# Two groups at a time in the attention layers of a graph network, and gated weights set up behind them

## The chip, the cores and the metric

The kernel runs on one core of one Trainium2 chip. The metric is the device time of one execution in microseconds (us), the median of three runs. A core has five engines with a queue of instructions each: TensorE (PE in the profile; PEld are its weight loads), VectorE (DVE), ScalarE (ACT), GpSimd (POOL) and SyncE (SP), which here starts the transfers.[...] TensorE writes into PSUM, which has eight banks of 128 x 512 floats; the other data stand in SBUF.

## The reference, cut to what matters

128 graphs of 128 nodes, 256 features per node. Three attention layers, then one gated layer of three steps, all with a residual:

```python
# three times, with layer's own W and a (the third also multiplies h' by nodemask)
h  = maximum(layernorm(x), 0)
Wh = einsum('bnf,fo->bno', h, W)
e  = (Wh @ a1)[:, :, None] + (Wh @ a2)[:, None, :]
e  = where(e > 0, e, 0.2 * e)
att = softmax(where(adj > 0, e, -9e15), axis=-1)
x  = x + elu(einsum('bij,bjo->bio', att, Wh))

# gated layer
h = maximum(layernorm(x), 0)
for i in range(3):
    m    = einsum('bnd,de->bne', h, weight[i])
    aggr = einsum('bst,bsd->btd', adj != 0, m)
    r = sigmoid(aggr @ w_ih_r.T + b + h @ w_hh_r.T + b)   # z in the same way
    n = tanh(aggr @ w_ih_n.T + b + r * (h @ w_hh_n.T + b))
    h = (1 - z) * n + z * h
x = x + h
```

All is float32.

## The kernel before

Four graphs make a group (G = 4, T = 512 columns); there are 32 groups. `gat(g)` is the attention part of a group, `gru(g)` its gated part. Both are generators, and the driver decides in which order the source emits their pieces. A framework builds the dependencies, and its scheduler orders the instructions on each engine; that order is fixed when the program is compiled, and each engine follows it. Pools give each tile a fixed number of buffers; a new tile waits until the last reader of the one that had its buffer is done.

```python
grp = ctx.enter_context(tc.tile_pool(name="grp", bufs=2))
gw = ctx.enter_context(tc.tile_pool(name="gw", bufs=2))
BANKS = {"gat": 3, "gru": 4, "tr": 1}          # the eight PSUM banks

loaded = {0: load(0)}                          # x and adj of group 0
# ... W of the three layers, with two more columns W @ a1 and W @ a2 (VectorE) ...
# ... nodemask, transposed (nmp) ...

def transposed(src, dst, nm_):                 # weights: load, transpose, copy
    t = su.tile([P, rows, D], FT, tag="wld", name=f"{nm_}_ld")
    nc.sync.dma_start(t, src.rearrange("(r p) d -> p r d", p=P))
    # ... nc.tensor.transpose into bank("gat"), nc.vector.tensor_copy out of it ...
transposed(w_hh, whh, "whh")
transposed(w_ih, wih, "wih")
for i in range(STEPS):
    transposed(gweight[i], gt, f"gt{i}")
    # wc[i] = gweight[i] @ w_ih.T: 8 matmuls of 384 columns (wcp), 4 copies by VectorE
# ... biases ...
```

One attention layer. The names are those of the profile:

```python
def attention(g, l, xt, cap):
    nm, rs = stats(xt, name)                   # VectorE statistics; rs: power on GpSimd
    for b in range(G):
        nc.scalar.activation(xn[:, b, :], xt[:, b, :], AF.Relu, bias=nm[:, b : b + 1])
    hT = turned(xn, gw, "hT", name)            # hTp: 8 transposes; k=0 copied by ScalarE, k=1 by VectorE
    yield
    for c in range(G):                         # whp: 2 matmuls of 258 columns each
        nc.tensor.matmul(ps[:, :E], hT[:, k, c * P : (c + 1) * P], W[l][:, k, :], ...)
        nc.scalar.activation(wh[:, c, :], ps[:, :E], AF.Copy, scale=rs[:, c : c + 1])
    yield
    # e: 4 transposes; em: 4 + 1 operations and nmx on VectorE; pe: 4 exponentials on
    # ScalarE; ri and pe * ri on VectorE
    xm = gw.tile([P, G, D], FT, tag="xm", name=f"xm_{name}")
    nc.gpsimd.tensor_scalar(xm, xt, 1.0, -1.0, op0=OP.mult, op1=OP.add)
    yield
    # atp: 4 transposes of pe, at: copied by VectorE
    xo = grp.tile([P, G, D], FT, tag=f"x{l + 1}", name=f"xo_{name}", bufs=3 if l == 2 else 2)
    for j in range(G // 2):                    # hp: 2 matmuls of 256 columns each
        nc.tensor.matmul(hp[:, b * D : (b + 1) * D], at[...], wh[:, c, :D], ...)
        nc.scalar.activation(t, hp, AF.Exp)
        nc.vector.scalar_tensor_tensor(u, hp, 0.0, xm[...], op0=OP.max, op1=OP.add)
        nc.vector.scalar_tensor_tensor(xo[...], t, 1.0, u, op0=OP.min, op1=OP.add)
    yield xo
```

After three layers `gat` makes the gated layer's first input (statistics, `hn`, eight transposes hTp). A gated step, for each half c of the features:

```python
if c == 0: evac(0)                             # hnp: 4 transposes of h in the bank "tr", hn: copied by ScalarE
for k in range(KD):
    mm(nn, cn, whh, h, k, ...); mm(pr, cr, whh, h, k, ...); mm(pz, cz, whh, h, k, ...)
    if c == 0:
        aggregate(k)                           # agp: 4 matmuls in the bank "tr", ag: copied by VectorE
        if k == 0: evac(1)
# wn; then r <- ag, n; ni <- ag, n, tanh; z <- ag; d, d, h: two matmuls of 512 columns
# for each gate, activations on ScalarE, five operations of 128x512 on VectorE
```

The driver:

```python
AHEAD = 2
for g in range(min(AHEAD, NG)):
    run(gat(g))
for g in range(NG):
    run(gru(g))
    if g + AHEAD < NG:
        run(gat(g + AHEAD))
```

In the profile a float32 matmul shows as two instructions (48 agp instructions in a group are 24 matmuls), a transpose as one.

Of the kernel before, what the change touches and what calls it, by code (L numbers as in the profile page):

```python
# [8 lines left out]
FT = mybir.dt.float32  # L9
I32 = mybir.dt.int32  # L10
AF = mybir.ActivationFunctionType
OP = mybir.AluOpType
AX = mybir.AxisListType

P = 128
# [6 lines left out]
def kernel(  # L22
# [24 lines left out]
    nc = tc.nc  # L47
    B, N, D = x.shape
    KD = D // P
    G = 4  # L50
# [16 lines left out]
    def load(g):  # L67
        xt = grp.tile([P, G, D], FT, tag="x0", name=f"x_{g}")
        nc.sync.dma_start(xt, x[g * G : (g + 1) * G].rearrange("b n d -> n b d"))
        at = grp.tile([P, G, N], I32, tag="adj", name=f"adj_{g}")  # L70
        nc.sync.dma_start(at, adj[g * G : (g + 1) * G].rearrange("b i j -> i b j"))
        return xt, at

    loaded = {0: load(0)}


    ident = const.tile([P, P], FT, name="ident")
# [25 lines left out]
    nc.tensor.transpose(nmp[:, :B], nm, ident[:B, :B])  # L103
    nmT = const.tile([P, B], FT, name="nmT")
    nc.vector.tensor_copy(nmT, nmp[:, :B])


    def transposed(src, dst, nm_):
        rows = src.shape[0] // P
        t = su.tile([P, rows, D], FT, tag="wld", name=f"{nm_}_ld")  # L110
        nc.sync.dma_start(t, src.rearrange("(r p) d -> p r d", p=P))
        for k in range(KD):
            for r0 in range(0, rows, 4):
                n = min(4, rows - r0)
                ps = bank("gat", f"{nm_}_{k}_{r0}")
                for r in range(n):
                    nc.tensor.transpose(
                        ps[:, r * P : (r + 1) * P], t[:, r0 + r, k * P : (k + 1) * P], ident
                    )
                nc.vector.tensor_copy(dst[:, k, r0 * P : (r0 + n) * P], ps[:, : n * P])  # L120

    O3 = w_ih.shape[0]
    NCH = O3 // P
    whh = const.tile([P, KD, O3], FT, name="whh")
    transposed(w_hh, whh, "whh")

    nc.vector.tensor_scalar_mul(whh[:, :, 2 * D :], whh[:, :, 2 * D :], 0.5)
    wih = su.tile([P, KD, O3], FT, tag="wih", name="wih", bufs=1)
    transposed(w_ih, wih, "wih")

    wc = []
    for i in range(STEPS):
        gt = su.tile([P, KD, D], FT, tag="gt", name=f"gt_{i}")
        transposed(gweight[i], gt, f"gt{i}")
        wci = const.tile([P, KD, O3], FT, name=f"wc_{i}")
        for m in range(KD):
            for o0 in range(0, O3, 384):
                ps = bank("gat", f"wcp_{i}_{m}_{o0}")
                for k in range(KD):
                    nc.tensor.matmul(  # L140
                        ps[:, :384], gt[:, k, m * P : (m + 1) * P], wih[:, k, o0 : o0 + 384],
                        start=(k == 0), stop=(k == KD - 1),
                    )
                nc.vector.tensor_copy(wci[:, m, o0 : o0 + 384], ps[:, :384])
        wc.append(wci)


    bi = const.tile([P, NCH], FT, name="bi")
    bh = const.tile([P, NCH], FT, name="bh")
    with nc.allow_non_contiguous_dma(reason="768 biases, once"):  # L150
        nc.sync.dma_start(bi, b_ih.rearrange("(c p) -> p c", p=P))
        nc.sync.dma_start(bh, b_hh.rearrange("(c p) -> p c", p=P))
    brz = const.tile([P, NCH], FT, name="brz")
    nc.vector.tensor_add(brz, bi, bh)
    nc.vector.tensor_scalar_mul(brz, brz, 0.5)
    nc.vector.tensor_scalar_mul(bh, bh, 0.5)

    setup.close()
    rw = ctx.enter_context(tc.tile_pool(name="rw", bufs=2))


    def stats(xt, name):
# [29 lines left out]
    def attention(g, l, xt, cap):  # L192

        name = f"{g}_{l}"
        nm, rs = stats(xt, name)

        xn = gw.tile([P, G, D], FT, tag="xn", name=f"xn_{name}")
        for b in range(G):
            nc.scalar.activation(xn[:, b, :], xt[:, b, :], AF.Relu, bias=nm[:, b : b + 1])
        hT = turned(xn, gw, "hT", name)  # L200
        yield

        wh = gw.tile([P, G, E], FT, tag="wh", name=f"wh_{name}")
        for c in range(G):
            ps = bank("gat", f"whp_{name}_{c}")
            for k in range(KD):
                nc.tensor.matmul(  # L207
                    ps[:, :E], hT[:, k, c * P : (c + 1) * P], W[l][:, k, :],
                    start=(k == 0), stop=(k == KD - 1),
                )  # L210
            nc.scalar.activation(wh[:, c, :], ps[:, :E], AF.Copy, scale=rs[:, c : c + 1])  # L211
        yield

        e2 = bank("gat", f"e2_{name}")
        for c in range(G):
            nc.tensor.transpose(  # L216
                e2[:, c * P : (c + 1) * P], wh[:, c, D + 1 : D + 2].to_broadcast([P, P]), ident
            )

        em = gw.tile([P, G, N], FT, tag="em", name=f"em_{name}")  # L220
        for c in range(G):
            nc.vector.scalar_tensor_tensor(  # L222
                em[:, c, :], e2[:, c * P : (c + 1) * P], wh[:, c, D : D + 1], cap[:, c, :],
                op0=OP.add, op1=OP.min,
            )
        nc.vector.scalar_tensor_tensor(em, em, ALPHA, em, op0=OP.mult, op1=OP.max)
        nmx = gw.tile([P, G], FT, tag="nmx", name=f"nmx_{name}")
        nc.vector.tensor_reduce(nmx, em, axis=AX.X, op=OP.max, negate=True)
        pe = gw.tile([P, G, N], FT, tag="pe", name=f"pe_{name}")
        sm = gw.tile([P, G], FT, tag="sm", name=f"sm_{name}")  # L230
        for b in range(G):
            nc.scalar.activation(  # L232
                pe[:, b, :], em[:, b, :], AF.Exp, bias=nmx[:, b : b + 1], accum_out=sm[:, b : b + 1]
            )
        ri = gw.tile([P, G], FT, tag="ri", name=f"ri_{name}")
        nc.vector.reciprocal(ri, sm)
        if l == 2:
            nc.vector.tensor_mul(ri, ri, nmT[:, g * G : (g + 1) * G])
        nc.vector.tensor_tensor(
            pe, pe, ri.rearrange("p (g o) -> p g o", o=1).to_broadcast([P, G, N]), op=OP.mult  # L240
        )

        xm = gw.tile([P, G, D], FT, tag="xm", name=f"xm_{name}")
        nc.gpsimd.tensor_scalar(xm, xt, 1.0, -1.0, op0=OP.mult, op1=OP.add)  # L244
        yield
        atp = bank("gat", f"atp_{name}")
        for b in range(G):
            nc.tensor.transpose(atp[:, b * P : (b + 1) * P], pe[:, b, :], ident)  # L248
        at = gw.tile([P, T], FT, tag="at", name=f"at_{name}")
        nc.vector.tensor_copy(at, atp)  # L250
        xo = grp.tile([P, G, D], FT, tag=f"x{l + 1}", name=f"xo_{name}", bufs=3 if l == 2 else 2)
        for j in range(G // 2):
            hp = bank("gat", f"hp_{name}_{j}")
            for b in range(2):
                c = 2 * j + b
                nc.tensor.matmul(  # L256
                    hp[:, b * D : (b + 1) * D], at[:, c * P : (c + 1) * P], wh[:, c, :D],
                    start=True, stop=True,
                )

            t = gw.tile([P, T], FT, tag="t", name=f"t_{name}_{j}")
            nc.scalar.activation(t, hp, AF.Exp)  # L262
            u = gw.tile([P, T], FT, tag="u", name=f"u_{name}_{j}")
            nc.vector.scalar_tensor_tensor(  # L264
                u, hp, 0.0, xm[:, 2 * j : 2 * j + 2, :].rearrange("p b d -> p (b d)"),
                op0=OP.max, op1=OP.add,
            )
            nc.vector.scalar_tensor_tensor(  # L268
                xo[:, 2 * j : 2 * j + 2, :].rearrange("p b d -> p (b d)"), t, 1.0, u,
                op0=OP.min, op1=OP.add,  # L270
            )
        yield xo

    done = {}

    def gat(g):
        xt, adj_t = loaded.pop(g)
        if g + 1 < NG:
            loaded[g + 1] = load(g + 1)
        cap = grp.tile([P, G, N], FT, tag="cap", name=f"cap_{g}")  # L280
        nc.vector.tensor_scalar(cap, adj_t, 0.0, 2.0 * BIG, op0=OP.is_gt, op1=OP.mult)
        nc.vector.tensor_scalar(cap, cap, -BIG, None, op0=OP.add)
        am = grp.tile([P, G, N], FT, tag="am", name=f"am_{g}", bufs=3)
        nc.vector.tensor_scalar(am, adj_t, 0.0, None, op0=OP.not_equal)
        for l in range(3):
            for v in attention(g, l, xt, cap):
                if v is not None:
                    xt = v
                yield
        nm, rs = stats(xt, f"{g}_3")  # L290
        nc.vector.tensor_mul(nm, nm, rs)
        hn = grp.tile([P, G, D], FT, tag="hn0", name=f"hn_{g}_0")
# [103 lines left out]
        nc.sync.dma_start(out[g * G : (g + 1) * G].rearrange("b n d -> n b d"), o)  # L396
        yield

    def run(stream):
        for _ in stream:  # L400
            pass

    AHEAD = 2
    for g in range(min(AHEAD, NG)):
        run(gat(g))
    for g in range(NG):
        run(gru(g))
        if g + AHEAD < NG:  # L410
            run(gat(g + AHEAD))


# [33 lines left out]
```

## Time and profile before

| | |
|---|---|
| time, median of 3 | 3158.22 us (3157.09 to 3161.38) |
| span of the profiled execution | 3155.9 us, 31261 instructions |
| TensorE busy | 3049.1 us (97%) |
| VectorE, ScalarE, GpSimd busy | 57%, 42%, 8% |
| memory traffic | 47.94 MB, mean 15 GB/s |

How to read it: the page gives each engine's busy time, and below it the span in 40 slices of 79 us with a digit each, 9 for 90% or more. PEclk is the clock that TensorE was granted, in tenths of full speed. In the timeline a row is a run of like instructions: start, length, engine, line, operation, tile written <- tiles read, shape, count, and in brackets the idle time of the engine before it with what ended it. An engine's idle time matters where that engine or what waits for it sets the end.

### The profile page before, as it was taken

How to read it: one execution, taken by the hardware profiler on the slowest of the kernel's cores; microseconds unless marked ns; L12 is line 12 of the kernel's file. 1: busy time of each engine (PE TensorE's matmuls, PEld its weight loads, DVE VectorE, ACT ScalarE, POOL GpSimd, SP SyncE). 2: the span in 40 equal slices, each digit the busy share in tenths (PEclk: the TensorE clock that was granted, in tenths of full speed). 3: DMA queues.
4: the chain of work that ended last, by engine and by line, in shares of the span. 5: the costliest groups of instructions: out<-in, count | busy, mean ns of one | idle time of the engine just before them, and what ended most of it. 6: DMA issues, size and time to landing. Idle time of an engine off the chain costs nothing.

```text
span 3155.9 us, 31261 instructions
## 1 busy us (share of the span) xinstructions
PE 3049.1 (97%) x11093; PEld 1730.8 (55%) x11093; DVE 1785.9 (57%) x3960; ACT 1316.4 (42%) x2881; POOL 262.3 (8%) x358
## 2 busy tenths in 40 slices
PE   5799999999999999999999999999999999999999
PEld 3455555555555555555555555555555555555554
DVE  4555565555655555655555655556555555555553
ACT  1344444444444444444444444444444444444442
POOL 0110100010101001100001100101000001010000
PEclk8899999999999999999999999999999999999999
DMA  2000000000000000000000000000000000000000
GB/s 84 11 17 17 11 7 17 17 17 13 15 7 17 17 17 10 14 11 17 17 17 11 7 17 17 17 17 10 7 17 17 17 11 17 7 14 7 7 1 14
DMA packets 56188, 47.94 MB, mean 15 GB/s; under 512 B 3296, under 2 KB 55648, under 8 KB 56032
## 3 DMA queue, kind: packets, MB, share of 16 engines
q1 hardware_dynamic: 56032, 45.95, 4.6%
q8 instruction: 87, 1.43, 0.2%
q14 instruction: 69, 0.57, 0.1%
HBM read 29.17 MB, written 16.78 MB: 15 GB/s over the span
## 4 chain that ended last, share of the span: by engine, by line
PE 79%; DVE 11%; ACT 6%; issue 3%; DMA 1%; POOL 0%; SPq 0%; ACTq 0%; DVEq 0%; POOLq 0%
PE r L321 18%; PE z L321 16%; PE whp L207 10%; PE nn L321 9%; PE ni L321 8%; PE agp L338 4%; PE hTp L183 4%; PE hp L256 4%; DVE st L167 3%; DVE u L264 3%; DVE xo L268 2%; PE hnp L312 2%; PE atp L248 2%; ACT pe L232 2%; PE e L216 1%
## 5 line engine op out<-in xcount | busy, mean ns | idle before, releaser
L321 PE MATMUL r<-ag,wc 128*128 128x512 f32 x768 | 381.3, 597 | 0.0
L321 PE MATMUL ni<-ag,wc 128*128 128x512 f32 x768 | 371.3, 592 | 0.0
L321 PE MATMUL z<-ag,wc 128*128 128x512 f32 x768 | 366.0, 592 | 0.0
L207 PE MATMUL whp<-w,hT 128*128 128x258 f32 x1536 | 361.5, 385 | 0.7 <-ACT hT L187 0.7
L207 PEld LDWEIGHTS whp<-w,hT 128*128 128x128 f32 x1536 | 286.8, 191 | 90.5 <-ACT hT L187 39.1
L222 DVE SCALAR_TENSOR_TENSOR em<-e,wh,cap 128x128 f32<-128x128 f32 x384 | 108.1, 344 | 397.3 <-PE e L216 397.3
L367 ACT ACTIVATE r<-r,brz 128x512 f32<-128x512 f32 x192 | 131.9, 687 | 457.5 <-PE r L321 457.5
L211 ACT ACTIVATE wh<-whp,rs 128x258 f32<-128x258 f32 x384 | 183.0, 477 | 264.9 <-PE whp L207 264.7
L369 DVE SCALAR_TENSOR_TENSOR n<-r,wn 128x512 f32<-128x512 f32 x192 | 130.7, 681 | 263.5 <-ACT r L367 263.5
L362 ACT ACTIVATE wn<-nn,bh 128x512 f32<-128x512 f32 x192 | 131.3, 684 | 326.4 <-PE nn L321 326.4
L321 PE MATMUL nn<-h,whh 128*128 128x512 f32 x512 | 264.8, 599 | 0.0
L321 PE MATMUL z<-h,whh 128*128 128x512 f32 x512 | 263.2, 595 | 0.1
L321 PE MATMUL r<-h,whh 128*128 128x512 f32 x512 | 261.6, 592 | 0.0
L338 PEld LDWEIGHTS agp<-am,hn 128*128 128x128 f32 x1536 | 203.3, 193 | 64.4 <-issue 47.6
L321 PEld LDWEIGHTS z<-ag,wc 128*128 128x128 f32 x768 | 143.5, 190 | 168.0 <-issue 167.9
L374 ACT ACTIVATE n<-n,bi 128x512 f32<-128x512 f32 x192 | 137.8, 718 | 233.6 <-DVE n L373 233.6
L244 POOL TENSOR_SCALAR xm<-xo 128x1024 f32<-128x1024 f32 x64 | 66.9, 1045 | 1965.4 <-DVE xo L268 1965.4
L321 PEld LDWEIGHTS ni<-ag,wc 128*128 128x128 f32 x768 | 140.8, 190 | 153.0 <-issue 153.0
L262 ACT ACTIVATE t<-hp 128x512 f32<-128x512 f32 x192 | 114.6, 597 | 263.4 <-PE hp L256 263.3
L264 DVE SCALAR_TENSOR_TENSOR u<-hp,xm 128x512 f32<-128x512 f32 x192 | 132.0, 688 | 149.8 <-ACT t L262 149.8
L338 PE MATMUL agp<-am,hn 128*128 128x128 f32 x1536 | 208.0, 275 | 0.0
L342 DVE COPY ag<-agp 128x512 f32<-128x512 f32 x192 | 130.9, 682 | 124.2 <-PE agp L338 124.2
(84 smaller groups left out, 4400.4 us busy)
## 6 DMA issues: line engine op xcount, KB each, us to landing
x<-in_x_dram SPq DMA_DIRECT2D x32, 512.0 KB, 3.9
out_dram<-o SPq DMA_DIRECT2D x32, 512.0 KB, 2.9
adj<-in_adj_dram SPq DMA_DIRECT2D x32, 256.0 KB, 2.8
w<-in_L_gnn_W_dram SPq DMA_DIRECT2D x3, 256.0 KB, 6.4
ab<-in_L_gnn_a_dram SPq DMA_DIRECT2D x3, 256.0 KB, 6.2
whh_ld<-in_L_gnn_w_hh_dram SPq DMA_DIRECT2D x1, 768.0 KB, 8.2
wih_ld<-in_L_gnn_w_ih_dram SPq DMA_DIRECT2D x1, 768.0 KB, 6.1
gt_ld<-in_L_gnn_weight_dram SPq DMA_DIRECT2D x3, 256.0 KB, 3.6
```

The costliest lines, as they stand in the source:

```text
L183: nc.tensor.transpose(ps[:, b * P : (b + 1) * P], v[:, b, k * P : (k + 1) * P], ident)
L207: nc.tensor.matmul(ps[:, :E], hT[:, k, c * P : (c + 1) * P], W[l][:, k, :], start=(k == 0), stop=(k == KD - 1),)
L211: nc.scalar.activation(wh[:, c, :], ps[:, :E], AF.Copy, scale=rs[:, c : c + 1])
L256: nc.tensor.matmul(hp[:, b * D : (b + 1) * D], at[:, c * P : (c + 1) * P], wh[:, c, :D], start=True, stop=True,)
L264: nc.vector.scalar_tensor_tensor(u, hp, 0.0, xm[:, 2 * j : 2 * j + 2, :].rearrange("p b d -> p (b d)"), op0=OP.max, op1=OP.add,)
L321: nc.tensor.matmul(ps, w[:, k, c * P : (c + 1) * P], v[k], start=start, stop=stop)
L338: nc.tensor.matmul(ps[:, b * P : (b + 1) * P], hn[k][b], am[:, b, :], start=True, stop=True)
L342: nc.vector.tensor_copy(t, ps)
L362: nc.scalar.activation(wn, nn, AF.Identity, bias=bh[:, cn : cn + 1])
L367: nc.scalar.activation(r, pr, AF.Tanh, bias=brz[:, cr : cr + 1], scale=0.5)
L369: nc.vector.scalar_tensor_tensor(n, r, 1.0, wn, op0=OP.add, op1=OP.mult)
L374: nc.scalar.activation(n, n, AF.Tanh, bias=bi[:, cn : cn + 1])
```

## The change

Two groups go through the attention layers together, a layer of the one and then a layer of the other, the second group half its way behind; and the gated layer's weights, which nothing in attention needs, are set up after the first attention layers instead of before them. It is meant to give TensorE work of one group while the other is in its softmax or its tail, and to start attention earlier. `attention` has no yields inside it any more, so that a piece is a whole layer. To make room for two groups, `xm` and `u` are gone: GpSimd writes x - 1 into the output tile, and VectorE works in place. `am` gets a fourth buffer, and inputs are loaded two groups ahead. PSUM banks and all other buffers stay as they are.

```diff
-    loaded = {0: load(0)}
+    loaded = {g: load(g) for g in range(2)}
     ...
-    def transposed(src, dst, nm_):          # and all the setup of whh, wih, wc, biases:
     ...                                     # moved as it is to the end
     def attention(g, l, xt, cap):
-        yield                               # three yields taken out
     ...
-        xm = gw.tile([P, G, D], FT, tag="xm", name=f"xm_{name}")
-        nc.gpsimd.tensor_scalar(xm, xt, 1.0, -1.0, op0=OP.mult, op1=OP.add)
-        yield
+        xo = grp.tile([P, G, D], FT, tag=f"x{l + 1}", name=f"xo_{name}", bufs=3 if l == 2 else 2)
+        nc.gpsimd.tensor_scalar(xo, xt, 1.0, -1.0, op0=OP.mult, op1=OP.add)
     ...
-            u = gw.tile([P, T], FT, tag="u", name=f"u_{name}_{j}")
-            nc.vector.scalar_tensor_tensor(u, hp, 0.0, xm[...], op0=OP.max, op1=OP.add)
-            nc.vector.scalar_tensor_tensor(xo[...], t, 1.0, u, op0=OP.min, op1=OP.add)
-        yield xo
+            u = xo[:, 2 * j : 2 * j + 2, :].rearrange("p b d -> p (b d)")
+            nc.vector.scalar_tensor_tensor(u, hp, 0.0, u, op0=OP.max, op1=OP.add)
+            nc.vector.scalar_tensor_tensor(u, t, 1.0, u, op0=OP.min, op1=OP.add)
+        return xo
     def gat(g):
-        if g + 1 < NG:
-            loaded[g + 1] = load(g + 1)
+        if g + 2 < NG:
+            loaded[g + 2] = load(g + 2)
     ...
-        am = grp.tile([P, G, N], FT, tag="am", name=f"am_{g}", bufs=3)
+        am = grp.tile([P, G, N], FT, tag="am", name=f"am_{g}", bufs=4)
     ...
         for l in range(3):
-            for v in attention(g, l, xt, cap):
-                if v is not None:
-                    xt = v
-                yield
+            xt = attention(g, l, xt, cap)
+            yield
     ...
-    AHEAD = 2
-    for g in range(min(AHEAD, NG)):
-        run(gat(g))
-    for g in range(NG):
-        run(gru(g))
-        if g + AHEAD < NG:
-            run(gat(g + AHEAD))
+    streams = {g: gat(g) for g in range(NG)}
+    def piece(g):
+        if g < NG:
+            next(streams[g])
+    for g in (0, 1, 0, 1, 0, 1, 0):         # three layers and the last step of group 0,
+        piece(g)                            # three layers of group 1
+    # ... setup of whh, wih, wc, biases ...
+    for g in (1, 2, 2):
+        piece(g)
+    for g in range(NG):
+        for _ in gru(g):
+            pass
+        for n in (g + 2, g + 3, g + 2, g + 3):
+            piece(n)
```

More of the change, by code (lines that the diff above doesn't have):

```diff
@@ L105 @@
     nc.vector.tensor_copy(nmT, nmp[:, :B])
-    def transposed(src, dst, nm_):
[L109 to L159, printed above, removed]
     def stats(xt, name):
@@ L250, in attention @@
         nc.vector.tensor_copy(at, atp)
-        xo = grp.tile([P, G, D], FT, tag=f"x{l + 1}", name=f"xo_{name}", bufs=3 if l == 2 else 2)
         for j in range(G // 2):
@@ L262, in attention @@
             nc.scalar.activation(t, hp, AF.Exp)
-            u = gw.tile([P, T], FT, tag="u", name=f"u_{name}_{j}")
[L264 to L271, printed above, removed]
-        yield xo
+            u = xo[:, 2 * j : 2 * j + 2, :].rearrange("p b d -> p (b d)")
+            nc.vector.scalar_tensor_tensor(u, hp, 0.0, u, op0=OP.max, op1=OP.add)
+            nc.vector.scalar_tensor_tensor(u, t, 1.0, u, op0=OP.min, op1=OP.add)
+        return xo
     done = {}
@@ L282, in gat @@
         nc.vector.tensor_scalar(cap, cap, -BIG, None, op0=OP.add)
-        am = grp.tile([P, G, N], FT, tag="am", name=f"am_{g}", bufs=3)
+        am = grp.tile([P, G, N], FT, tag="am", name=f"am_{g}", bufs=4)
         nc.vector.tensor_scalar(am, adj_t, 0.0, None, op0=OP.not_equal)
         for l in range(3):
-            for v in attention(g, l, xt, cap):
-                if v is not None:
-                    xt = v
-                yield
+            xt = attention(g, l, xt, cap)
+            yield
         nm, rs = stats(xt, f"{g}_3")
@@ L397, in gru, with transposed @@
         yield
-    def run(stream):
-        for _ in stream:
-            pass
-    AHEAD = 2
-    for g in range(min(AHEAD, NG)):
-        run(gat(g))
-    for g in range(NG):
-        run(gru(g))
-        if g + AHEAD < NG:
-            run(gat(g + AHEAD))
+    streams = {g: gat(g) for g in range(NG)}
[4 more added lines that the diff above has]
+        piece(g)
+    def transposed(src, dst, nm_):
+        rows = src.shape[0] // P
+        t = su.tile([P, rows, D], FT, tag="wld", name=f"{nm_}_ld")
+        nc.sync.dma_start(t, src.rearrange("(r p) d -> p r d", p=P))
+        for k in range(KD):
+            for r0 in range(0, rows, 4):
+                n = min(4, rows - r0)
+                ps = bank("gat", f"{nm_}_{k}_{r0}")
+                for r in range(n):
+                    nc.tensor.transpose(
+                        ps[:, r * P : (r + 1) * P], t[:, r0 + r, k * P : (k + 1) * P], ident
+                    )
+                nc.vector.tensor_copy(dst[:, k, r0 * P : (r0 + n) * P], ps[:, : n * P])
@@ new lines @@
+    O3 = w_ih.shape[0]
+    NCH = O3 // P
+    whh = const.tile([P, KD, O3], FT, name="whh")
+    transposed(w_hh, whh, "whh")
+    nc.vector.tensor_scalar_mul(whh[:, :, 2 * D :], whh[:, :, 2 * D :], 0.5)
+    wih = su.tile([P, KD, O3], FT, tag="wih", name="wih", bufs=1)
+    transposed(w_ih, wih, "wih")
+    wc = []
+    for i in range(STEPS):
+        gt = su.tile([P, KD, D], FT, tag="gt", name=f"gt_{i}")
+        transposed(gweight[i], gt, f"gt{i}")
+        wci = const.tile([P, KD, O3], FT, name=f"wc_{i}")
+        for m in range(KD):
+            for o0 in range(0, O3, 384):
+                ps = bank("gat", f"wcp_{i}_{m}_{o0}")
+                for k in range(KD):
+                    nc.tensor.matmul(
+                        ps[:, :384], gt[:, k, m * P : (m + 1) * P], wih[:, k, o0 : o0 + 384],
+                        start=(k == 0), stop=(k == KD - 1),
+                    )
+                nc.vector.tensor_copy(wci[:, m, o0 : o0 + 384], ps[:, :384])
+        wc.append(wci)
@@ new lines @@
+    bi = const.tile([P, NCH], FT, name="bi")
+    bh = const.tile([P, NCH], FT, name="bh")
+    with nc.allow_non_contiguous_dma(reason="768 biases, once"):
+        nc.sync.dma_start(bi, b_ih.rearrange("(c p) -> p c", p=P))
+        nc.sync.dma_start(bh, b_hh.rearrange("(c p) -> p c", p=P))
+    brz = const.tile([P, NCH], FT, name="brz")
+    nc.vector.tensor_add(brz, bi, bh)
+    nc.vector.tensor_scalar_mul(brz, brz, 0.5)
+    nc.vector.tensor_scalar_mul(bh, bh, 0.5)
+    setup.close()
+    rw = ctx.enter_context(tc.tile_pool(name="rw", bufs=2))
```

## The prediction

> **What bounds the kernel now.** I read the first page for the engine that is nearly always busy, and for where in the span it is not.
>
> ```profile
> PE 3049.1 (97%) x11093; PEld 1730.8 (55%) x11093; DVE 1785.9 (57%) x3960; ACT 1316.4 (42%) x2881; POOL 262.3 (8%) x358
> ...
> PE   5799999999999999999999999999999999999999
> ...
> PEclk8899999999999999999999999999999999999999
> ```
>
> TensorE is full in 38 of 40 slices; only the first two are loose, and there its clock is lower too. So the most that a better order can win lies in the first 115 us and in small stalls later. Next the busy time by stretch, cut where setup ends (39.87 us) and where the first gated matmuls begin to fill TensorE (114.44 us); the columns are length, busy time and instructions of PE, PEld, DVE, ACT, POOL, clock, DMA share, GB/s.
>
> ```profile
> 0.00:39.87 39.87, 23.94 (x86) 15.41 (x86) 21.32 (x71) 2.99 (x5) 3.12 (x9) 1.00 0.57 167
> 39.87:114.44 74.57, 38.46 (x129) 27.18 (x128) 31.53 (x83) 21.92 (x59) 8.16 (x11) 0.71 0.01 4
> 114.44:3061.00 2946.56, 2898.65 (x10618) 1645.84 (x10618) 1698.13 (x3755) 1268.03 (x2783) 251.05 (x338) 1.00 0.04 14
> 3061.00:3156.00 95.00, 88.06 (x265) 42.41 (x263) 34.95 (x51) 23.49 (x35) 0.00 (x0) 0.99 0.03 11
> ```
>
> The second stretch is the three attention layers of group 0 alone: TensorE works half the time, at a clock of 0.71. The third is the steady part: per group there are (11093 - 85) / 32 = 344 TensorE instructions (85 belong to the setup), so it holds 10618 / 344 = 30.9 groups of 95.5 us. How full is it? Busy times overlap, so I take start-to-start times from the timeline of TensorE:
>
> ```profile
> 1588.30 1.05 PE L338 MATMUL agp<-am,hn 128*128 128x128 f32 x8
> 1589.19 1.02 PE L321 MATMUL nn<-h,whh 128*128 128x512 f32 x2
> 1590.05 1.02 PE L321 MATMUL r<-h,whh 128*128 128x512 f32 x2
> 1590.90 1.02 PE L321 MATMUL z<-h,whh 128*128 128x512 f32 x2
> 1593.17 0.66 PE L312 MATMUL hnp<-ident,h 128*128 128x128 f32 x4 [1.24 <-DVE ag L342]
> ```
>
> Two instructions of 512 columns start every 0.86 us, so 0.43 each; of 128 columns 0.11; the 258-column ones follow at 0.218 and the 256-column ones at 0.217. A group's floor is 144 x 0.43 + (48 agp + 80 transposes) x 0.11 + 48 x 0.218 + 24 x 0.217 = 61.9 + 14.1 + 10.5 + 5.2 = 91.7 us. The steady loss is 95.5 - 91.7 = 3.8 us a group. Of it 1.4 is the one stall in the last line above (z should end at 1591.76, hnp starts at 1593.17): VectorE copied `ag` only behind three tail operations and three statistics of an attention layer. The rest is some fifteen stalls of 0.05 to 0.36.
>
> Last, TensorE in an attention layer of the head, with the wait before each piece in brackets:
>
> ```profile
> 61.23 2.15 PE L183 MATMUL hTp<-ident,xn 128*128 128x128 f32 x8 [4.42 <-ACT xn L199]
> 63.63 5.75 PE L207 MATMUL whp<-w,hT 128*128 128x258 f32 x16 [0.25 <-ACT hT L187]
> 69.21 0.49 PE L216 MATMUL e<-ident,wh 128*128 128x128 f32 x3
> 69.94 0.32 PE L216 MATMUL e<-ident,wh 128*128 128x128 f32 x1 [0.24 <-ACT wh L211]
> 75.64 1.09 PE L248 MATMUL atp<-ident,pe 128*128 128x128 f32 x4 [5.37 <-DVE pe L239]
> 77.51 3.78 PE L256 MATMUL hp<-wh,at 128*128 128x256 f32 x8 [0.78 <-DVE at L250]
> ```
>
> Two holes per layer: 5.4 us of softmax, 4.4 to 5.1 us of tail and statistics. From hTp to hTp a layer takes 25 us (61.23 to 86.39).
>
> **The Trainium skill.** (1) "TensorE: Matmul & The Clock Gate", Part 1: an idle window of about 3.4 us halves the TensorE clock, and a busy one restores it. The trace agrees: after the 5.4 us hole hp takes 3.78 us for x8, in the steady part 1.89 to 1.99. (2) "Perfetto Trace Analysis", Identifying the Most-Contended Engine: matmul busy share is a bad measure of distance to the peak. Agrees: means of 592 ns against starts 430 ns apart, which is why I count starts. (3) "PSUM — Partial Sum Buffer", Engine vs sequencer instructions: the other engines' queues are strict FIFO and matmuls start in program order. Agrees with the 1.24 us above, where a ready `agp` waited behind other VectorE work. So the compiled order decides what can fill a hole.
>
> **Part 1: the head, with setup behind attention.** The source asks for layers of groups 0 and 1 in turn. The compiled TensorE queue does not interleave them inside a layer (one layer per line, 0L1 = group 0, layer 1):
>
> ```
> 0L0: hTp whp e | atp hp     1L0: hTp whp e | atp hp     0L1: ... 1L1: ... 0L2: ...
> 1L2: hTp whp e agp(group 0) | atp hp     hTp of group 0's last step
> whh wih transposes, nn, gt, r, wcp x16, gt, z, wcp x16, gt, nn, wcp x16, hTp of group 1 ...
> ```
>
> At each bar nothing stands in the queue to fill the softmax wait (one aggregation in the last). Only the second hole, tail and statistics, is covered. Step by step:
> - Start. Before, the first hTp is at 39.87, behind setup. After, 0.77 MB more (x and adj of group 1) stands ahead of the weights. The 2.9 MB up to w_hh had landed by 13.1 us, so nodemask, first in TensorE's queue, comes at about 13.5 instead of 11.0. The third attention vector, loaded when the first is used up (10.07 to 14.19 before), lands near 17, and VectorE's evacuation of hT stands behind its products: about 19.5, against 41.6 before. Layer 0L0 then ends 11.9 us after the end of its whp (44.9 to 56.8 before): whp near 23.5, end near 35.5.
> - Five more layers. hTp starts as the other group's hp ends; 1.6 us to whp, 3.7 at full clock, 1.1 to the end of e, 5.4 hole, 1.1 atp, 0.8 wait, hp 1.8 to 3.6: 15.5 to 17.4 us. The 5.4 us hole can still drop the clock, so 16.8: 5 x 16.8 = 84, end at about 119.5.
> - Setup behind it: 26.3 us before (13.1 to 39.4). It keeps its own waits on VectorE copies and weight loads, but 3.4 us of gated matmuls stand in them, and hTp comes first: saturated from about 119.5 + 1 + 27 = 147.5.
>
> Ledger at that point, in full-clock TensorE time: setup 48 x 0.32 + 37 x 0.11 = 19.5; an attention group 3 x (16 x 0.11 + 16 x 0.218 + 8 x 0.217) + 0.9 = 21.9. Before: at 114.44 done 19.5 + 21.9 = 41.4, lost 73. After: at 147.5 done 19.5 + 21.9 + 21.0 + 4.3 = 66.7, lost 81. Part 1 costs about 8 us: six layers at 17 in a row are no shorter than three at 25 plus three hidden for nothing in the steady part, where TensorE was full anyway.
>
> **Part 2: the steady order.** Per group the queue holds the same 344 instructions, in one repeating order. Walking it with the durations above: the 1.4 us stall goes, because `ag` of step 1 now stands right behind the four `em` (1.04 + 0.68 us after e, while nn and r take 1.7). New ones come where one group's tail meets the next group's layer: whp 0.4 (third "gat" bank free only 2.1 us after hp, 1.7 us of matmuls between); the last e 0.6 (ScalarE does `wh` behind `hn`, which waits for GpSimd's power, 1.04 us); hTp 0.5 (paced by xn); whp 0.3 (hT evacuation behind a tanh). Small ones as before, about 1.9. Sum 3.7 against 3.8: a gain of 0.1 to 0.2 a group, x 29 = about 5 us.
>
> **Part 3: in place.** u and xm become the output tile; the counts and shapes on VectorE (690 ns each) and GpSimd (1045 ns) stay. GpSimd's copy must now wait for an older x tile, but it has 8% to do. Zero. The last two groups run without attention as before: zero.
>
> Sum: 3158 + 8 - 5 = 3161.
>
> **Rivals.** (A) The idea works: both holes filled, two groups' layers in some 75 us together with part of setup. Before lost 73 in the head; with about 20 lost to the first loads and 10 to setup, 43 come back: about 3115. For it: the holes are there and the work is independent. Against: the compiled order has nothing at the bar. (B) The steady order is worse than my walk: each 1 us more per group costs 29 us; with two such, 3219. For it: in-order VectorE and ScalarE now serve a tail, another group's layer and the gated step at once. Against: only one attention stream's worth of work per group, and VectorE is 57% busy. (C) The steady order is better: only small stalls of 0.1 remain, 2 us a group, 29 x 1.8 = 52 less: 3110. For it: the largest stall is certainly gone.
>
> **Range and chances.** The head is good to about 8 us either way, the walk to 0.7 us a group or 20 us. Together some 22; 8 in 10 is 3132 to 3190. The 2% line is at 63 us: to reach it downward, A and C would have to hold almost fully together, upward, B with its two microseconds. 3% each; 94% within.
>
> **What would show it.** Right: TensorE waits of 5 us on `pe` six times in the head; saturated at 140 to 155 us; the clock in the head between 0.7 and 0.9; the 37.5 us of hnp waiting for `ag` down to a few; a steady group of 95 to 96 us. Wrong: hTp of one group between e and atp of the other on the chip; a layer under 14 us; a period off 95.5 by more than 1, with a wait of whp, e or hTp on ScalarE that recurs 29 times.

## The result and the profile after

| | before | after |
|---|---|---|
| time, median | 3158.55 us | 3137.37 us |
| ratio | | 0.9931, 95% interval 0.9914 to 0.9949 |
| span of the profiled execution | 3155.9 us | 3134.2 us |
| end of a group's output to the next, steady part | 95.58 us | 94.61 us |
| last addition for the first group's output starts | 213.5 us | 235.5 us |

The change is worth 21 us, 0.7%. The forecast was 3161 in a range of 3132 to 3190. The page of after, the lines that answer to those of before:

```profile
PE 3057.9 (98%) x11093; PEld 1721.3 (55%) x11093; DVE 1807.1 (58%) x3960; ACT 1309.9 (42%) x2881; POOL 263.8 (8%) x358
...
PE   5799999999999999999999999999999999999999
...
PEclk8899999999999999999999999999999999999999
```

In slices it looks like before: no shorter head can be seen. The stretches, cut at the first instruction of TensorE, at the end of the six attention layers, at the end of setup and where the last two groups begin (columns as in the prediction):

```profile
0.00:12.61 12.61, 0.00 (x0) 0.03 (x1) 7.85 (x29) 2.99 (x5) 4.34 (x10) 1.00 0.82 254
12.61:123.66 111.05, 66.96 (x249) 50.54 (x250) 58.90 (x163) 40.36 (x113) 14.08 (x18) 0.81 0.12 34
123.66:150.12 26.46, 25.86 (x101) 15.73 (x100) 18.31 (x49) 4.86 (x10) 2.53 (x4) 0.97 0.16 50
150.12:3039.00 2888.88, 2876.98 (x10482) 1612.54 (x10481) 1687.12 (x3672) 1238.21 (x2718) 242.89 (x326) 1.00 0.04 13
3039.00:3134.20 95.20, 88.06 (x265) 42.42 (x263) 34.94 (x51) 23.49 (x35) 0.00 (x0) 0.97 0.03 11
```

Six layers take 111 us, setup 26 us stands behind them in full, and TensorE is saturated only from 150 us. From there to 3039 TensorE's idle time (length less busy time) is nearly gone: 12 us of 2889, where before had 48 of 2947. Busy times overlap, so this is not the whole loss: by start times a group still takes 94.6 us for a floor of 91.7. One layer of the head, TensorE alone:

```profile
53.53 1.14 PE L129 MATMUL hTp<-ident,xn 128*128 128x128 f32 x8
54.96 3.75 PE L152 MATMUL whp<-w,hT 128*128 128x258 f32 x16 [0.29 <-ACT hT L133]
58.55 0.49 PE L160 MATMUL e<-ident,wh 128*128 128x128 f32 x3
59.28 0.32 PE L160 MATMUL e<-ident,wh 128*128 128x128 f32 x1 [0.24 <-ACT wh L156]
65.56 1.08 PE L191 MATMUL atp<-ident,pe 128*128 128x128 f32 x4 [5.96 <-DVE pe L183]
67.43 3.63 PE L198 MATMUL hp<-wh,at 128*128 128x256 f32 x8 [0.78 <-DVE at L193]
70.90 1.04 PE L129 MATMUL hTp<-ident,xn 128*128 128x128 f32 x8
```

The last row is the other group's layer: the hole in front of hTp is closed, the one in front of atp is not, and behind it TensorE is slow (hp at 3.63 us, against 1.99 in the steady part; the granted clock is 0.81 in these layers). All of TensorE's waits, in total, times, longest:

```profile
PE atp L191 <- DVE pe L183: 32.6, 6, 6.0
PE nmp L103 <- DMA nm<-in_nodemask_dram: 12.6, 1, 12.6
PE e L160 <- ACT wh L156: 11.6, 34, 0.4
PE hp L198 <- DVE at L193: 4.7, 6, 0.8
```

The 37.5 us of hnp behind `ag` are gone; in their place stands a new, smaller wait of the last e for `wh`, once per group.

### The profile page after: what moved, and what is told of

Read it like the earlier page. It is cut to its first block, busy times and chain, and to the rows that moved or that the text cites. A ratio compares the mean times of both kernels' runs of the same rounds, so it can differ in the third digit from the quotient of the medians.

```text
span 3134.2 us, 31156 instructions
## 1 busy us (share of the span) xinstructions
PE 3057.9 (98%) x11093; PEld 1721.3 (55%) x11093; DVE 1807.1 (58%) x3960; ACT 1309.9 (42%) x2881; POOL 263.8 (8%) x358
## 4 chain that ended last, share of the span: by engine, by line
issue 49%; PE 36%; DVE 8%; POOL 4%; ACT 2%; DMA 0%; POOLq 0%; DVEq 0%; ACTq 0%
PE r L255 8%; PE z L255 6%; PE whp L152 4%; PE nn L255 4%; PE hp L198 3%; PE ni L255 3%; POOL rs L120 3%; PE hTp L129 2%; PE agp L272 2%; DVE xo L207 1%; DVE xo L206 1%; DVE st L113 1%; DVE d L316 1%; PE atp L191 1%; PE hnp L246 1%
## 5 line engine op out<-in xcount | busy, mean ns | idle before, releaser
L152 PE MATMUL whp<-w,hT 128*128 128x258 f32 x1536 | 371.8, 388 | 4.1 <-ACT hT L133 3.4
L152 PEld LDWEIGHTS whp<-w,hT 128*128 128x128 f32 x1536 | 278.2, 191 | 106.4 <-DVE hT L135 31.3
L255 PEld LDWEIGHTS r<-ag,wc 128*128 128x128 f32 x768 | 128.5, 190 | 149.8 <-issue 78.2
L198 PE MATMUL hp<-wh,at 128*128 128x256 f32 x768 | 201.8, 407 | 4.7 <-DVE at L193 4.7
L198 PEld LDWEIGHTS hp<-wh,at 128*128 128x128 f32 x768 | 144.1, 198 | 92.0 <-DVE at L193 74.3
L206 DVE SCALAR_TENSOR_TENSOR xo<-hp,xo 128x512 f32<-128x512 f32 x192 | 132.0, 687 | 108.7 <-ACT t L204 108.5
```

Of the source, the lines that this page charges most:

```text
L198: nc.tensor.matmul(hp[:, b * D : (b + 1) * D], at[:, c * P : (c + 1) * P], wh[:, c, :D], start=True, stop=True,)
L206: nc.vector.scalar_tensor_tensor(u, hp, 0.0, u, op0=OP.max, op1=OP.add)
L255: nc.tensor.matmul(ps, w[:, k, c * P : (c + 1) * P], v[k], start=start, stop=stop)
```

## Experiments

Each was timed beside the kernel before on the same chip. "Period" is the time from one group's output to the next in the middle of the span.

**In place alone.** Kernel before, with this part of the change alone (cut):

```diff
-        xm = gw.tile([P, G, D], FT, tag="xm", ...)
-        nc.gpsimd.tensor_scalar(xm, xt, 1.0, -1.0, ...)
+        xo = grp.tile([P, G, D], FT, tag=f"x{l + 1}", ...)
+        nc.gpsimd.tensor_scalar(xo, xt, 1.0, -1.0, ...)
-            u = gw.tile([P, T], FT, tag="u", ...)
+            u = xo[:, 2 * j : 2 * j + 2, :].rearrange("p b d -> p (b d)")
```

> The kernel before with only the third part of the change: u and xm go, GpSimd and VectorE work in the output tile. Theory (the 0.93 us per group come from where the second group's layers stand in the queues): nothing changes, 3158 us within 4, 95.5 us from one group's output to the next, TensorE still waits about 37 us in total for hnp behind the copy ag. Rival (fewer tiles and GpSimd's early copy loosen the queues): period near 94.6, about 3130 us.

Measured 3155.3 us, ratio 0.9987 (0.9981 to 0.9994), period 95.49; hnp still waits 37.5 us for `ag`. In place is worth 0.1 us a group, some 3 to 4 us in all: not the source of the gain.

**One group at a time.** Kernel after:

```diff
-    for g in (0, 1, 0, 1, 0, 1, 0):
+    for g in (0, 0, 0, 0):
     ...                                     # setup stays between
-    for g in (1, 2, 2):
+    for g in (1, 1, 1, 1):
     ...
-        for n in (g + 2, g + 3, g + 2, g + 3):
+        for n in (g + 2, g + 2, g + 2, g + 2):
```

> The kernel after, but one group at a time: all of group 0, setup, all of group 1, then after each gated group all of group g+2. Setup behind attention and in place stay. Theory: period 95.5 again, head as long as before (setup only changes places with three layers), 3155 to 3165 us. Rival (setup behind attention or in place gives the gain): 3130 to 3140 us.

Measured 3150.8 us, 0.9972 (0.9961 to 0.9983), period 95.46, and hnp waits for `ag` again:

```profile
PE hnp L246 <- DVE ag L276: 37.2, 30, 1.2
```

It is 4 us below the theory's range: attention starts earlier, and the first output comes at 210.1 us, in the last experiment at 213.9. So of the period's 0.97 us, 0.85 come from taking two groups together. Another offset than half a way was not tried.

**Setup first.** Kernel after, the setup block moved back ahead of the first layers, as it is.

> The kernel after with the setup of the gated weights ahead of all attention again. Theory: setup stands on the path in either place, so 3137 to 3142 us, the period stays 94.6; the six layers in a row stand later by some 20 us and setup's 25 us behind them are gone. Rival (setup behind attention is worth its transfers, and the early start shows): 3150 us or more.

Measured 3140.2 us, 0.9938 (0.9923 to 0.9953), period 94.62. The 3 us to after lie within the two intervals: setup is on the path in either place.

**Setup in other banks.** Kernel after:

```diff
-                ps = bank("gat", f"{nm_}_{k}_{r0}")
+                ps = bank("gru", f"{nm_}_{k}_{r0}")
-                ps = bank("gat", f"wcp_{i}_{m}_{o0}")
+                ps = bank("gru", f"wcp_{i}_{m}_{o0}")
```

> The kernel after; the setup takes its PSUM tiles from the four banks of the gated part, which are idle in the head, instead of from the three that attention takes in turn. Theory (the bank order ties setup behind attention): setup goes into the softmax holes; of the 24.7 us from the first whh transpose to the end of setup some 21 come back (3.4 were gated matmuls): 3114 to 3120 us. Rival (the holes are not free: VectorE copies of setup delay the attention chain, or the clock falls no less): 3130 to 3140 us.

Measured 3115.2 us, 0.9860 (0.9846 to 0.9875). With the order of the source untouched, the scheduler now puts setup where it belongs. TensorE in the first softmax hole:

```profile
25.26 0.82 PE L160 MATMUL e<-ident,wh 128*128 128x128 f32 x3
25.90 0.40 PE L354 MATMUL whh<-ident,whh_ld 128*128 128x128 f32 x2
26.14 0.27 PE L160 MATMUL e<-ident,wh 128*128 128x128 f32 x1
26.25 1.26 PE L354 MATMUL whh<-ident,whh_ld 128*128 128x128 f32 x10
...
30.35 0.88 PE L354 MATMUL wih<-ident,wih_ld 128*128 128x128 f32 x6 [0.75 <-DVE whh L357]
...
32.70 1.05 PE L191 MATMUL atp<-ident,pe 128*128 128x128 f32 x4 [0.25 <-DVE pe L183]
34.53 3.78 PE L198 MATMUL hp<-wh,at 128*128 128x256 f32 x8 [0.78 <-DVE at L193]
```

Between e and atp stand whh, wih and gt; atp waits 0.25 us in place of 5.4. The holes of the first three layers are filled so; then setup is used up, and the next two atp wait 5.4 and 5.8 us again. As nothing but the pool was changed, it was the three banks shared with attention that kept setup behind it. The likely way, read from the queues and not tested by itself: a pool's buffers go round in the order in which the source asks for them, so what asks later cannot go first. Whether more "gat" banks would also let two layers pass one another was not tried.

**Half layers in the head.** Kernel after, a yield before atp (`half(g)` is one such piece), and for the first layers:

```diff
-    for g in (0, 1, 0, 1, 0, 1, 0):
-        piece(g)
+    for g in (0, 1, 0, 0, 1, 1, 0, 0, 1, 1, 0, 0, 1):
+        half(g)
```

> The kernel after; in the head alone the two groups alternate by half layers (up to the softmax, and from its transposes on), so that one group's first half stands in the queue between e and atp of the other. Setup stays behind. Theory (a layer emitted whole takes the three banks in turn and locks the hole): two layers take about 25 us instead of 2 x 17.5, so the last hp ends about 28 us earlier, 3105 to 3113 us. Rival (VectorE and ScalarE are the chain, two streams slow each other): 30 us or more per pair, 3125 us or more.

Measured 3135.0 us, 0.9924 (0.9910 to 0.9939), far from the 3105 to 3113 of the theory. The softmax holes closed, and another opened:

```profile
PE hTp L129 <- ACT xn L145: 23.0, 4, 6.0
PE nmp L103 <- DMA nm<-in_nodemask_dram: 13.2, 1, 13.2
PE e L160 <- ACT wh L156: 10.8, 30, 0.5
PE hTp L129 <- ACT hn L231: 8.5, 2, 7.5
```

The list puts group 0's next first half right behind its second half, so hTp stands in the queue with nothing ahead of it for the time of tail and statistics. Two layers still took 35 us, 17.5 each, as in after.

**Both.** The last two edits together.

> Half layers in the head and setup in the banks of the gated part, together. Theory: the gains add, less what the smaller holes cannot take: TensorE saturated near 100 us, 3085 to 3095 us. Rival: the two fillings want the same holes, no better than the better one alone, about 3110 us.

Measured 3116.8 us, 0.9869 (0.9852 to 0.9885): the banks' gain and nothing of the halves. A hole that moves is no gain.

**Half layers throughout.** As before it, and in the steady part `for n in (0, 1, 0, 1, 1, 0, 1): half(g + 2 + n)` after each gated group.

> As the last one, and half layers in the steady part too. Theory: TensorE has gated matmuls for every hole there, so the period changes only by the accidents of the VectorE and ScalarE order: 94 to 95.5 us, 3075 to 3120 us. Rival (what hides holes in the head hides them in the steady part too): period near its floor of 91.7 to 93, 3010 to 3050 us.

Measured 3096.7 us, 0.9802 (0.9788 to 0.9817), period 93.87. 20 us less than the last one, by 0.74 us per group. The period is a little below the theory's 94 to 95.5; the rival's 91.7 to 93 was not reached. The wait of e for `wh`, 0.36 us a group in after, is gone from the steady part; what makes up the rest of the 0.74 is not shown.

**Half layers in pairs.** Kernel after, with the halves in another order:

```diff
-    for g in (0, 1, 0, 1, 0, 1, 0):
-        piece(g)
+    for g in (0, 1) * 6 + (0,):
+        half(g)
```

> The kernel after; in the head the half layers now go first half of group 0, first half of group 1, second half of 0, second half of 1, so that neither the softmax nor the tail of one group stands alone in the queue. (The earlier split put group 0's next first half right behind its second half: the softmax holes closed, and waits of 5 to 6 us on xn opened, with two layers still 35 us.) Theory: two layers in some 24 us, 3102 to 3112 us. Rival (two streams cannot go faster than 35 us a pair, for VectorE and ScalarE): 3125 us or more.

Measured 3114.7 us, 0.9861 (0.9847 to 0.9876), 23 us below after, 3 us above the expectation. A pair takes 26.6 us (hTp of group 0 at 44.67 and at 71.22 us), not 24, for a remainder of the hole is left in front of the second group's atp:

```profile
61.05 1.99 PE L199 MATMUL hp<-wh,at 128*128 128x256 f32 x8 [1.27 <-DVE at L194]
66.00 0.86 PE L192 MATMUL atp<-ident,pe 128*128 128x128 f32 x4 [2.95 <-DVE pe L183]
67.65 3.78 PE L199 MATMUL hp<-wh,at 128*128 128x256 f32 x8 [0.78 <-DVE at L194]
```

**All of `ag` on ScalarE.** Kernel before, in `aggregate`:

```diff
-                nc.vector.tensor_copy(t, ps)
+                nc.scalar.copy(t, ps)
```

> The kernel before with one edit: ScalarE copies ag out of PSUM instead of VectorE, so that it does not stand behind an attention tail in VectorE's queue. Theory (that stall of 1.4 us is where the steady part lost against after): the 37 us of hnp behind ag go to nearly zero, period 94.0 to 94.6, 3112 to 3130 us. Rival (the wait only moves to another place in the order): the 37 us go, the period stays above 95.3, 3150 us or more.

Measured 3148.5 us, 0.9968 (0.9956 to 0.9981), period 95.24. Between the two theories: the 37 us are gone, but hTp now waits for `xn` and `hn` on ScalarE, 0.8 and 0.6 us in a group on average. As ScalarE got 3.4 us more to do, this alone doesn't say why; hence the next.

**One `ag` on ScalarE.** Kernel before, the late copy alone:

```diff
-                nc.vector.tensor_copy(t, ps)
+                if (i, k) == (1, 0):
+                    nc.scalar.copy(t, ps)
+                else:
+                    nc.vector.tensor_copy(t, ps)
```

> The kernel before; of the six copies of ag in a group only the one that was late (step 1, first half) goes to ScalarE, so that ScalarE gets 0.6 us per group more and not 3.4. Theory A (the stall of 1.4 us at hnp is a loss by itself): period 94.0 to 94.4, 3112 to 3125 us. Theory B (the stall hid another wait: one group at a time puts the next layer's hTp too few matmuls behind the same group's hp, and its xn comes only after tail and statistics): the stall at hnp goes, hTp waits about 1 us for xn instead, period 95.0 to 95.5, 3142 to 3158 us.

Measured 3158.1 us, 0.9996 (0.9987 to 1.0004), period 95.52: Theory B for the time. The same stretch of a layer on TensorE as in the prediction:

```profile
1588.66 1.99 PE L256 MATMUL hp<-wh,at 128*128 128x256 f32 x8
...
1592.24 0.64 PE L312 MATMUL hnp<-ident,h 128*128 128x128 f32 x4
...
1594.43 1.05 PE L338 MATMUL agp<-am,hn 128*128 128x128 f32 x8
1596.57 0.44 PE L183 MATMUL hTp<-ident,xn 128*128 128x128 f32 x2 [1.08 <-ACT xn L199]
```

hnp no longer waits, and the time is paid four rows further down. In the steady part hTp waits 22.9 us for `xn` and 17.9 us for `hn`, 29 times each: 1.4 us a group, for the 1.25 that hnp waited. From hp to the next layer's hTp it is 7.9 us here (8.1 in before); TensorE has 6.5 us to do in between, whatever their order.

Theory B says that tail and statistics take the rest, and that is not all of it. `xn` waits for `nm` (the negated means, VectorE's last operation of the statistics), and `nm` ends with a copy by GpSimd on which it does not depend. Here, and below it in before:

```profile
1594.90 1.04 POOL L244 TENSOR_SCALAR xm<-x 128x1024 f32<-128x1024 f32 x1
1595.18 0.79 DVE L170 TENSOR_SCALAR nm<-mv 128x4 f32<-128x4 f32 x1
...
1592.43 1.04 POOL L244 TENSOR_SCALAR xm<-x 128x1024 f32<-128x1024 f32 x1
1593.24 0.27 DVE L170 TENSOR_SCALAR nm<-mv 128x4 f32<-128x4 f32 x1
```

Apart from such copies `nm` takes 0.14 to 0.17 us; so some 0.6 of the 1.08 us are this delay. VectorE reached `nm` earlier with the copy of `ag` gone, and GpSimd held it. In the run with in place alone no `nm` of 128 took over 0.17. The two edits together, in place and this copy on ScalarE, were not run; whether the stall's 1.25 us would then be worth something is open.

**Pairs and banks.** Half layers in pairs, and setup in the banks of the gated part.

> The pairs of half layers, and setup in the banks of the gated part. Theory: setup's 21 us and the pairs' 30 us add up as long as holes remain: 3084 to 3096 us. Rival (they want the same holes): no better than 3103 us.

Measured 3096.4 us, 0.9803 (0.9789 to 0.9818): 41 us below after, close to the sum of 22 and 23, and 0.4 us above what was expected. There is room for both fillings.

**All together.** With the steady order of half layers too.

> As the last one, with the half layers in the steady order that gave a period of 93.87: 0.74 us less for each of 28 to 29 groups, 20 to 22 us below the last one, 3063 to 3076 us. Rival (head and steady order disturb one another): within 10 us of the last one.

Measured 3076.1 us, 0.9739 (0.9724 to 0.9753), period 93.93: 20 us below the last one, as expected, 2.6% faster than before, about 2% than after. Its head, columns as above:

```profile
0.00:40.00 40.00, 20.49 (x99) 15.99 (x99) 26.23 (x86) 13.38 (x37) 6.09 (x13) 1.00 0.59 172
40.00:80.00 40.00, 32.55 (x130) 23.56 (x131) 28.94 (x81) 17.48 (x47) 10.82 (x14) 0.83 0.03 8
80.00:120.00 40.00, 37.16 (x173) 26.01 (x172) 27.27 (x78) 20.27 (x52) 4.60 (x7) 1.00 0.09 27
120.00:160.00 40.00, 39.91 (x140) 21.91 (x139) 28.69 (x67) 19.20 (x45) 5.94 (x7) 1.00 0.00 1
```

Between 40 and 120 us TensorE runs 303 instructions and is busy for 69.7 of 80 us.

## Why the prediction was right, point by point, and where it was off

- *What bounds the kernel*: right. In every version the time follows from TensorE's holes in the head and from the period.
- *No interleaving inside a layer*: right; six waits for `pe`, 32.6 us, the clock 0.81 in that stretch. The prediction did not name the cause. For setup it is the three banks, as the run with other banks shows; for the layers of two groups the order of the source was enough to change it (half layers in pairs), and the part of the banks is argued.
- *Start*: whp of the first layer was to end near 23.5; e starts at 23.9.
- *Five more layers at 16.8*: 17.6 by the trace (35.75 to 123.66). The clock was low behind each hole, hp took 3.6 to 3.8.
- *Setup behind it, 28 with hTp (1 + 27)*: 26.5. Saturated at 150.1, not 147.5; lost 150.1 - 66.7 = 83, not 81. By this count part 1 costs 10 us where 8 were predicted. One group's two layers are done ahead of time, which is why the first output is 22 us late and the last gap but one 15.7 us shorter (79.6 for 95.3).
- *The steady order*: the direction was right, and this term was mis-sized. A loss of 3.7 us per group was worked out for after; 94.6 - 91.7 = 2.9 was measured. Of the four new stalls the e behind `hn` is 0.52 by start times (0.6), hTp paced by xn 0.36 (0.5), the third bank 0.12 (0.4), the evacuation behind a tanh none above 0.05 (0.3). The gain of 0.97 us in 29 gaps between outputs is 28.2 us where 5 were predicted.
- *The sum*: told by the outputs it closes. The first comes 21.9 us later, the last gap but one is 15.7 shorter, the 29 gaps before it 28.2: the last output comes 22.0 us earlier. The head thus costs 6 us; where the 4 us lie by which the count at 150 us says more is not assigned. The forecast of 3161 was 3 us above before, and 3137 is 21 below, 5 us above the lower end of the range: nearly all of the 24 us between them is the steady order. That the number fell inside the range it owes to the range's width.
- *The signs named*: all as for "right" (the six waits are 4.1 to 6.0 us) but one: the steady group takes 94.6 us and not 95 to 96.
- *Why the 1.4 us go*: incomplete. The prediction put them down to `ag` behind VectorE's tail and three statistics (in before's trace four are ahead of it). That wait was real, but freeing it alone gave nothing: behind it lay the wait for the next layer's `xn`, itself held up by `nm`, and one for `hn`. That taking two groups together is what counts is shown by the run with one group at a time. How it works is read from the order, not shown by a run: in after, the next hTp of the same group follows hp directly only once in three times (0 to 1, 8.3 us apart, a stall of 0.36); layer 2 follows layer 1 half a gated group later, and the last step follows layer 2 after another group's layer.
- *In place*: zero was predicted; 0.1 us per group was measured. It is the size by which `nm` was drawn out in before (0.27 for 0.17 us); that this is the cause is not shown.
- *Rivals*: A was out for the kernel as written, but its mechanism holds once order or banks allow it. C came true by half: 2.9 us of loss, not 2.

## What to carry to other kernels

Before work is reordered to fill a hole, look at the buffers: a small pool shared by two streams can tie their order. Here a change of pool alone was worth 22 us, as much as the whole reordering. Remove a stall and look for the wait that it hid: follow the chain from one layer's last matmul to the next one's first, on every engine that it touches, and compare it with the work that stands between them in the queue. When two streams alternate, each cut must have work of the other stream behind it, or the hole only moves.

## What the hardware showed beside that

In the run with pairs hp took 3.78 us each of the three times that atp had waited 2.9 to 3.0 us, and 1.99 after a wait of 1.27. But the length of the last hole does not decide it. With half layers in the head, hp was slow after a wait of 1.26:

```profile
33.33 3.68 PE L199 MATMUL hp<-wh,at 128*128 128x256 f32 x8 [1.26 <-DVE at L194]
```

And with setup in other banks, hp at 34.53 took 3.78 us although in the 8 us before it TensorE ran transposes with no wait over 0.78. So a filled hole did not always keep the clock; what decides is not shown here.

Transposes follow the clock too: in after, four atp take 1.09 us behind the hole of the head and 0.60 in the steady part, with `pe` ready before the first in both.

VectorE's `nm` (128x4) takes 0.14 to 0.17 us, but in before, and in the two runs with `ag` on ScalarE, 31 of 128 take 0.26 to 0.80 and end 0.02 to 0.03 us after a copy of 128x1024 by GpSimd, though nothing in the source ties them. The averages of `mv` in the same stretch are not drawn out (0.18 us at most). Why one operation is held and the other is not, no run here shows.
